# Nine full units a group of heads, and heads' rows laid out by DMA, in the first attention of a four-layer model

## The chip, the cores and the metric

The kernel runs on one core of a Trainium2 chip. The metric is the device time of one execution in microseconds. Before the change it is 3598.34 us, the median of three runs (3597.46 to 3599.22).

TensorE (PE) multiplies matrices and its weight loads are shown apart (PEld); VectorE is DVE, ScalarE is ACT, GpSimd is POOL; SyncE (SP) issues the DMAs. Everything is in float32, except one mask that is added by bfloat16 matmuls.

## The reference, cut to what matters

The model adds eight layers to x of 4 batches x 1024 positions x 128 features. The change lies in the first one, an attention with 16 heads of width 8, whose scores are a sum of four terms:

```python
v = (x @ v_w + v_b).reshape(Bq, Sq, H, Hd).transpose(0, 2, 1, 3)
...
scores = jnp.take(causal_kern, jnp.maximum(doff, 0), axis=-1)
qm = (x @ qmod_w + qmod_b).transpose(0, 2, 1)
km = (x @ kmod_w + kmod_b).transpose(0, 2, 1)
scores = scores + qm[..., :, None] + km[..., None, :]
qc = (x @ cq_w).reshape(Bq, Sq, H, CR).transpose(0, 2, 1, 3)
kc = (x @ ck_w).reshape(Bq, Sq, H, CR).transpose(0, 2, 1, 3)
scores = scores + MIX * jnp.einsum('bhic,bhjc->bhij', qc, kc) / math.sqrt(CR)
scores = jnp.where(causal, scores, -1000000000.0)
attn = jax.nn.softmax(scores, axis=-1)
ctx = jnp.einsum('bhij,bhjd->bhid', attn, v)
```

The first term depends on the distance of two positions alone (a table per head and batch). qm and km are one number per head and position, the modulations.

## The kernel before, in words

`attn0` first makes the table of the distance term (`position_table`), and then `attn0_heads` does the attention. A **group** is 4 heads of one batch, so there are 16 groups. Heads lie 32 rows apart: head h of a group has rows 32h to 32h+31 of a 128-row tile. Row 0 to 7 are the content of queries or keys, rows 8 and 9 the modulations against ones, and row 10 the shift of the softmax. So four matmuls of 32 rows each, one per head, run side by side on PE, and one product gives all of a score but the distance term.

The projections are therefore *gapped*: the weights `wq` and `wk` hold a head's 8 columns and its modulation in 32 columns with zeros between. For each group `queries(i)` (L669, evicted by ACT L671) and `keys(i)` (L675, L677) project the halves i = 0, 1 of 512 positions. Keys come from a transposed x with the positions reversed inside each half (`reverse`, `xr`), queries from a plain transpose (`turn`, `xT`).

The work of a group goes in **slots**. A slot has

- a *top*, which finds the maxima of scores without the distance term: four matmuls (L690 for the diagonal blocks, L705 for the others) into two pairs of PSUM banks, and two maximum reductions on DVE (L722). Diagonal blocks are masked first, by adding a lower value with the bfloat16 product of an identity and `after` (L698). The ten tops of a group are the list `tops`: both diagonals, `own` 3 and 7 (384 columns each), `both` 2 and 1 (a query tile in both halves; 512 and 256 columns), and four `before` (512). When a half's maxima are there, `maxima` is filled (L725), and `shift(i)` transposes it (L731) and adds it to the query rows (L732).
- *contract* of the unit three slots back (LAG = 3): the weights times the values (L787) into one bank, in which a whole half is summed and copied out by ACT at its end (L797).
- *weigh* of the unit nine slots back (LEAD = 9): scores of a key tile against all later queries of a half (L745) into two more pairs, the exponentials of heads 0 and 1 (L754) and of head 2 (L758) on ACT, the distance term of head 3 added on DVE (L757) ahead of its own exponential (L761). The other three heads get the distance term as a factor on POOL (L778), after a triangle is cut off in the diagonal block (L768). The ten units of a group are (0: 0), (0: 1 and 3), (0: 2), (1: 0) to (1: 4), (1: 5 and 7), (1: 6), written as half: key tiles. Eight have 512 columns, two have 256.
- *extras*, put into slots by hand with `at(slot, f)`: shift, queries, keys, for a new batch turn, reverse, values, and at a batch's end divide (L623 to L630), turn_back (L642), output (L649). All use the single bank `mm`, of which there is one.

PSUM has three pairs (tile `s`), one sum (`av`) and one single (`mm`). The order on PE, DVE and ACT is the written order (`manual_schedule`); POOL and SP are ordered by the framework. `fetch` loads a group's distance table (2 MB, two DMAs on SP, L665) in the first slot of the group into one of two buffers. Ahead of the slots, the first batch is transposed and the first group projected. What is left of the layer (`rest`) begins in the last slots.

Of the kernel before, what the change touches and what calls it, by code (L numbers as in the profile page):

```python
# [70 lines left out]
def gapped(w, width, at):  # L71

    k = w.shape[0]
    out = np.zeros((k, H, 32), np.float32)
    out[:, :, at : at + width] = w.reshape(k, H, width)
    return out.reshape(k, H * 32)


def head_columns(a):

    return np.asarray(a, np.float32).reshape(4, 4, 32).transpose(1, 2, 0).reshape(P, 4)


def layout(i):
# [41 lines left out]
    w.add("wq", gapped(a["cq_w"], 8, 0))  # L126
    w.parts[-1].reshape(P, H, 32)[:, :, 9] = a["qmod_w"]
    w.add("wk", gapped(a["ck_w"], 8, 0))
    w.parts[-1].reshape(P, H, 32)[:, :, 8] = a["kmod_w"]
    scale = np.ones((4, 32), np.float32)  # L130
    scale[:, :8] = 0.15 / np.sqrt(8.0)
    w.add("sq", scale.reshape(P, 1))
    bq = np.zeros((H, 32), np.float32)
    bq[:, 8] = 1.0
    bq[:, 9] = a["qmod_b"]
    w.add("bq", head_columns(bq))
    bk = np.zeros((H, 32), np.float32)
    bk[:, 8] = a["kmod_b"]
    bk[:, 9:11] = 1.0
    w.add("bk", head_columns(bk))  # L140
# [107 lines left out]
def hybrid_kernel(ctx: ExitStack, tc: tile.TileContext, x, out, blocks, dram, upto=8):  # L248
# [295 lines left out]
    def attn0_heads(W, xn, table, rest):  # L544
# [7 lines left out]
        LEAD, LAG = 9, 3  # L552

        tops = [("diagonal", 0), ("own", 3), ("both", 2), ("both", 1), ("diagonal", 1)]
        tops += [("before", it) for it in range(4, 8)] + [("own", 7)]

        units = [(i, jts) for i in range(2) for jts in [(jt,) for jt in range(4 * i + 1)] + [(4 * i + 1, 4 * i + 3), (4 * i + 2,)]]
        N = len(units)
        with layer_pool("a0h", 2) as pool, layer_pool("a0k", 1) as keep:

            maxima = [keep.tile([P, 4, P], F32, name=f"maxima{n}") for n in range(2)]
# [3 lines left out]
            parts = keep.tile([P, 2, 4, 4, 3], F32, name="parts")  # L565
            nc.gpsimd.memset(parts, -LOWEST)
            for n in range(2):
                nc.gpsimd.memset(maxima[n], 0.0)
                nc.gpsimd.memset(vals[n], 1.0)
# [14 lines left out]
            class Batch:  # L584
# [5 lines left out]
                def turn(self, i):  # L590
                    if i == 0:
                        self.xT = pool.tile([P, S], F32, name="xT", bufs=1)
                    ps = free()
                    for t in range(4):
                        nc.tensor.transpose(ps[:, t * P : (t + 1) * P], self.x[:, 4 * i + t, :], ident)
                    move(self.xT[:, i * 512 : (i + 1) * 512], ps)

                def reverse(self, i):

                    if i == 0:  # L600
                        self.xr = {}
                    ps = free()
                    for t in range(4):
                        mm(ps[:, (3 - t) * P : (4 - t) * P], self.x[:, 4 * i + t, :], flip, start=True, stop=True)
                    self.xr[i] = pool.tile([P, 512], F32, name=f"xr{i}", bufs=1)
                    move(self.xr[i], ps)
                    if i == 1:

                        nc.gpsimd.tensor_tensor(self.x, self.x, wide(shared, TB), ALU.add)
# [8 lines left out]
                def divide(self, t):  # L618
# [5 lines left out]
                    if t % 4 == 0:  # L624
                        self.o[i] = pool.tile([P, 4, H, 8], F32, name=f"o{i}", bufs=1)
# [13 lines left out]
                def turn_back(self, i):  # L639
# [3 lines left out]
                    self.oT[i] = pool.tile([P, 512], F32, name="oT")  # L643
# [9 lines left out]
            class Group:  # L653


                def __init__(self, batch, g):
                    self.batch, self.g = batch, g
                    self.q, self.k = {}, {}
# [8 lines left out]
                def queries(self, i):  # L667
                    ps = free()
                    mm(ps, W("wq")[:, self.g * P : (self.g + 1) * P], self.batch.xT[:, i * 512 : (i + 1) * 512], start=True, stop=True)  # L669
                    self.q[i] = pool.tile([P, 512], F32, name=f"q{i}")  # L670
                    nc.scalar.activation(self.q[i], ps, AF.Identity, bias=W("bq")[:, self.g : self.g + 1], scale=W("sq"))  # L671

                def keys(self, i):
                    ps = free()
                    mm(ps, W("wk")[:, self.g * P : (self.g + 1) * P], self.batch.xr[i], start=True, stop=True)  # L675
                    self.k[i] = pool.tile([P, 512], F32, name=f"k{i}")
                    nc.scalar.activation(self.k[i], ps, AF.Identity, bias=W("bk")[:, self.g : self.g + 1])  # L677

                def top(self, kind, n):
# [3 lines left out]
                    i = n if kind == "diagonal" else n // 4  # L683
                    t = n % 4
                    if kind == "diagonal":

                        for t in range(4):
                            for h in range(4):
                                r = slice(32 * h, 32 * h + 32)
                                mm(  # L690
                                    both[h // 2][:, h % 2, t * P : (t + 1) * P],
                                    self.q[i][r, t * P : (t + 1) * P],
                                    self.k[i][r, (3 - t) * P : (4 - t) * P],
                                    start=(t == 0),
                                    stop=False,
                                )
                        for h in range(4):
                            mm(both[h // 2][:, h % 2, :], ident16, wide(after, 4), start=False, stop=True)  # L698
                    else:
                        w = 512 if kind == "before" else t * P  # L700
                        for c, half in enumerate((0, 1) if kind == "both" else (i,)):
                            keys = self.k[0 if kind == "before" else half]
                            for h in range(4):
                                r = slice(32 * h, 32 * h + 32)
                                mm(  # L705
                                    both[h // 2][:, h % 2, c * w : (c + 1) * w],
                                    self.q[half][r, t * P : (t + 1) * P],
                                    keys[r, 512 - w : 512],
                                    start=True,
                                    stop=True,  # L710
                                )
                    for hp in range(2):
                        if kind == "diagonal":
                            o = parts[:, i, :, 2 * hp : 2 * hp + 2, 0].rearrange("p t h -> p h t")
                            x = both[hp].rearrange("p k (t w) -> p k t w", t=4)
                        elif kind == "both":
                            o = parts[:, :, t, 2 * hp : 2 * hp + 2, 1].rearrange("p i h -> p h i")
                            x = both[hp][:, :, 0 : 2 * w].rearrange("p k (i w) -> p k i w", i=2)
                        else:
                            o = parts[:, i, t, 2 * hp : 2 * hp + 2, 1 if kind == "own" else 2]  # L720
                            x = both[hp][:, :, 0:w]
                        nc.vector.tensor_reduce(o, x, AX.X, ALU.max, negate=True)  # L722
                    if (kind, n) in (tops[3], tops[-1]):
                        i = int((kind, n) == tops[-1])
                        nc.vector.tensor_reduce(maxima[i][:, :, 10:P:32], parts[:, i], AX.X, ALU.min)  # L725

                def shift(self, i):

                    ps = bank()
                    for t in range(4):  # L730
                        nc.tensor.transpose(ps[:, t * P : (t + 1) * P], maxima[i][:, t, :], ident)  # L731
                    return lambda: nc.vector.tensor_tensor(self.q[i], self.q[i], ps, ALU.add)  # L732

                def weigh(self, i, jts):

                    parted, w = [], 0
                    for jt in jts:
                        w0 = max(0, jt * P - 512 * i)
                        parted.append((jt, w0, slice(w, w + 512 - w0), 512 * i + w0 - jt * P))
                        w += 512 - w0  # L740
                    both = [pair().rearrange("p (k w) -> p k w", k=2) for _ in range(2)]
                    for jt, w0, c, u in parted:
                        for h in range(4):
                            r = slice(32 * h, 32 * h + 32)
# [11 lines left out]
                    for jt, w0, c, u in parted:  # L756
# [6 lines left out]
                    def bias():  # L763
                        for jt, w0, c, u in parted:
# [15 lines left out]
                    def contract():  # L780
                        ended = jts == (4 * i + 2,)
                        if jts[0] == 0:
                            self.acc = psum.sums()
                        for jt, w0, c, u in parted:
                            for h in range(4):
                                col = 16 * (4 * self.g + h)
                                mm(  # L787
                                    self.acc[32 * h : 32 * h + 32, w0:512],
                                    vals[self.batch.n][:, jt, col : col + 32],
                                    pt[:, h, c] if h < 3 else p3[:, c],  # L790
                                    start=(jt == 0),
# [1403 lines left out]
```

## Time and profile before

| | |
|---|---|
| time, median of three runs | 3598.34 us |
| the profiled execution: span from the first to the last instruction | 3593.0 us |
| what lies around the span (median less span) | 5.3 us |
| PE, DVE, ACT, POOL busy over the span | 95%, 57%, 55%, 26% |
| first top of the first group starts | 85.80 us |
| first exponential of the first unit (L754) starts | 112.47 us |
| last top reduced | 771.9 us |
| last first exponential starts | 808.35 us |
| L778 POOL, distance factor, 128x1536 (96 of the 192) | 3.44 us each |
| L722 DVE, maxima of 1024 columns | 1.21 us each, two a top |
| L754, L758, L761 ACT, 1024, 512, 512 columns | 1.02, 0.59, 0.63 us |
| L669, L675 PE, 60 projections in the slots, two instructions each | 1.02 to 1.12 us a projection |

The profiled execution has no time of its own beside its span; the three runs of the same kernel lie within 0.05% of each other. A line of the timeline reads: start, duration, engine, line, operation, what it writes and reads, shape, count of instructions, and in brackets how long the engine was idle before and who released it. Float32 matmuls are two instructions each, and four of them, on four groups of rows, run at the same time, so "x8, 1.07" is four matmuls of 512 columns side by side.

### The profile page before, as it was taken

To read this page: it belongs to the slowest core of one execution; us is meant where nothing else is said; L and a number is where in the kernel's file an instruction comes from. 1 tells how busy PE (TensorE), PEld (TensorE's weight loads), DVE (VectorE), ACT (ScalarE), POOL (GpSimd) and SP (SyncE) were. 2 spreads that over 40 slices of the span, in tenths; PEclk is the share of its full clock that TensorE was granted. 3 is DMA by queue.
4 is the path that set the end of the run, shared out by engine and by line. 5 is a ranking of instruction groups with operands and counts; after the bars stand their busy time and mean duration, and the time that the engine had idled before them with its cause. 6 is when DMAs were issued, how large, how long until landed. Compare 5 with 4: busy or idle time off the path is not lost.

```text
span 3593.0 us, 62577 instructions
## 1 busy us (share of the span) xinstructions
PE 3425.7 (95%) x25672; PEld 2041.0 (57%) x25672; DVE 2060.6 (57%) x4874; ACT 1959.1 (55%) x3284; POOL 916.5 (26%) x705
## 2 busy tenths in 40 slices
PE   7999999989999999999899999999999999999999
PEld 3444444436765566633333577666766766766777
DVE  5767767767644455577778411566566566566311
ACT  5455555556522225477677553566566566566543
POOL 4687878782022210122221000000001001000000
PEclk7999999999999999999999999999999999999999
DMA  3111111100520005200000000210010110100000
GB/s 98 50 48 48 48 48 48 48 24 23 147 61 1 1 15 142 72 1 1 1 1 1 14 1 1 72 36 29 32 36 25 36 36 25 36 25 24 4 10 13
DMA packets 95975, 124.34 MB, mean 35 GB/s; under 512 B 3660, under 2 KB 78028, under 8 KB 94536
## 3 DMA queue, kind: packets, MB, share of 16 engines
q1 hardware_dynamic: 95688, 120.33, 10.9%
q8 instruction: 202, 3.31, 0.4%
q14 instruction: 85, 0.70, 0.1%
HBM read 117.59 MB, written 2.73 MB: 33 GB/s over the span
## 4 chain that ended last, share of the span: by engine, by line
PE 83%; ACT 6%; DVE 6%; POOL 2%; DMA 1%; issue 1%; SPq 0%; ACTq 0%; DVEq 0%; POOLq 0%
PE mm L2040 8%; PE s L1990 8%; PE av L1827 6%; PE mm L1817 6%; PE av L2058 6%; PE s L745 5%; PE s L1653 4%; PE s L705 4%; PE av L787 4%; PE av L1148 3%; PE av L1687 3%; PE mm L1132 2%; ACT p L2025 2%; DVE p L1664 2%; PE av L1383 2%; PE mm L1347 2%
## 5 line engine op out<-in xcount | busy, mean ns | idle before, releaser
L778 POOL TENSOR_TENSOR p<-p,bias 128x1536 f32<-128x1536 f32 x192 | 503.2, 2629 | 64.5 <-ACT p L758 59.2
L2008 DVE CUSTOM_DVE_ANT_0 p<-s,bias 128x512 f32<-128x512 f32 (+3 forms) x768 | 387.0, 550 | 128.6 <-PE s L1990 121.5
L722 DVE TENSOR_REDUCE parts<-s 128x2 f32<-128x1024 f32 (+4 forms) x320 | 342.4, 1113 | 161.8 <-PE s L705 94.7
L2025 ACT ACTIVATE p<-p,tops 128x128 f32<-128x128 f32 (+7 forms) x512 | 395.2, 774 | 2.0 <-DVE tops L2008 1.8
L1664 DVE TENSOR_SCALAR p<-s 128x1024 f32<-128x1024 f32 (+1 forms) x320 | 340.8, 1110 | 82.3 <-PE s L1653 72.8
L2045 ACT COPY pt<-mm 128x512 f32<-128x512 f32 (+1 forms) x352 | 185.8, 528 | 364.2 <-PE mm L2040 364.0
L2040 PE MATMUL mm<-ident,p 128*128 128x128 f32 x2304 | 348.1, 283 | 30.7 <-ACT p L2025 30.3
L2040 PEld LDWEIGHTS mm<-ident,p 128*128 128x128 f32 x2304 | 248.3, 141 | 168.2 <-issue 63.4
L2073 POOL COPY wide_rec<-rec 128x512 f32<-128x512 f32 x64 | 39.4, 616 | 1163.0 <-DVE rec L2071 1098.7
L1667 ACT ACTIVATE p<-p 128x2048 f32<-128x2048 f32 (+1 forms) x160 | 277.6, 1740 | 93.7 <-DVE p L1664 93.1
L1827 PEld LDWEIGHTS av<-wt,hid 128*128 128x128 f32 x2048 | 263.9, 192 | 107.1 <-issue 107.1
L1990 PE MATMUL s<-keys,q 64*128 64x512 f32 (+3 forms) x1536 | 302.2, 512 | 4.5 <-DVE tops L2008 4.5
L754 ACT ACTIVATE p<-s 128x1024 f32<-128x1024 f32 (+1 forms) x160 | 150.3, 939 | 265.6 <-PE s L745 261.9
L2058 PE MATMUL av<-pt,vals 128*64 128x128 f32 x4608 | 294.7, 277 | 0.0
L1818 ACT ACTIVATE hid<-mm,wt 128x512 f32<-128x512 f32 x256 | 170.7, 690 | 219.2 <-PE mm L1817 218.9
L2058 PEld LDWEIGHTS av<-pt,vals 128*64 128x64 f32 x4608 | 248.4, 137 | 51.4 <-issue 40.8
L1827 PE MATMUL av<-wt,hid 128*128 128x128 f32 x2048 | 264.7, 275 | 0.0
L2047 DVE COPY pt<-mm 128x512 f32<-128x512 f32 (+1 forms) x288 | 189.6, 658 | 129.7 <-PE mm L2040 129.4
L1817 PE MATMUL mm<-xT,wt 128*128 128x512 f32 x512 | 260.2, 599 | 2.5 <-ACT hid L1818 2.0
L1653 PE MATMUL s<-q,k 32*128 32x512 f32 (+3 forms) x1536 | 209.9, 533 | 2.2 <-DVE p L1664 2.0
L745 PE MATMUL s<-q,k 32*128 32x512 f32 (+3 forms) x1536 | 197.4, 529 | 0.5 <-DVE parts L722 0.4
L1148 PEld LDWEIGHTS av<-wt,hid 128*128 128x128 f32 x1152 | 154.6, 200 | 60.5 <-issue 53.1
(405 smaller groups left out, 5282.4 us busy)
## 6 DMA issues: line engine op xcount, KB each, us to landing
root<-roots SPq DMA_DIRECT2D x128, 256.0 KB, 6.2
bias<-rel_dram SPq DMA_DIRECT2D x32, 1024.0 KB, 5.4
bias<-pos_dram SPq DMA_DIRECT2D x16, 1536.0 KB, 7.1
bias<-pos_dram SPq DMA_DIRECT2D x16, 512.0 KB, 7.9
wt<-w_ffn SPq DMA_DIRECT2D x2, 2132.0 KB, 8.0
wt<-w_ffn SPq DMA_DIRECT2D x2, 1192.0 KB, 5.2
wt<-w_attn SPq DMA_DIRECT2D x1, 2336.0 KB
x_sb<-x SPq DMA_DIRECT2D x4, 512.0 KB, 6.8
```

The costliest lines, as they stand in the source:

```text
L722: nc.vector.tensor_reduce(o, x, AX.X, ALU.max, negate=True)
L745: mm(both[h // 2][:, h % 2, c], self.k[jt // 4][r, (3 - jt % 4) * P : (4 - jt % 4) * P], self.q[i][r, w0:512], start=True, stop=True,)
L778: nc.gpsimd.tensor_tensor(d, d, self.bias[:, 0:3, u : u + 512 - w0], ALU.mult)
L1653: mm(both[h // 2][:, h % 2, c : c + 512 - w0], self.k[r, jt * P : (jt + 1) * P], self.q[r, 512 * i + w0 : 512 * (i + 1)], start=True, stop ...
L1664: nc.vector.tensor_scalar(pt[:, 2 * hp : 2 * hp + 2, 0:w], both[hp][:, :, 0:w], 80.0, -80.0, ALU.min, ALU.max)
L1817: mm(ps, W("w1")[:, c * P : (c + 1) * P], self.batch.xT[:, self.i * 512 : (self.i + 1) * 512], start=True, stop=True)
L1827: mm(o, self.hid[:, c, t * P : (t + 1) * P], W("w2")[:, c * P : (c + 1) * P], start=(c == 0), stop=(c == C - 1))
L1990: mm(s[:, kk, 0:e], self.q[r, it * P : (it + 1) * P], keys[self.n][r, S - n + c : S - n + c + e], start=True, stop=True,)
L2008: nc.vector.tensor_tensor_reduce(out=self.p[it][:, kk, c : c + e], in0=s[:, kk, 0:e], in1=self.bias[:, kk, c : c + e], scale=-1.0, scalar= ...
L2025: nc.scalar.activation(p, p, AF.Exp, bias=self.top[it][:, kk : kk + 1], scale=-1.0, accum_out=self.sums[:, it, kk : kk + 1])
L2040: nc.tensor.transpose(ps[:, m, kk, :], self.p[it][:, kk, (m0 + m) * P : (m0 + m + 1) * P], ident)
L2058: mm(self.acc[64 * kk : 64 * kk + 64, (it % 4) * P : (it % 4 + 1) * P], vals[self.n][:, it - m0 - m, :], pt[:, m, kk, :], start=(m0 + m == 0),
```

## The change

1. **Nine units and nine tops a group.** The half units are joined: (0: 2) and (1: 6) become one unit of 512 columns. The contraction of (1: 6) is held until the second half has been begun by (1: 0). The tops are cut by query tiles over whole causal rows: `row` is one tile's 512 columns, `rows` a tile of 384 and one of 128 columns, `both` two of 256 columns. Keys are reversed within a half, so the masked block is the first 128 columns of each piece, and masks are 128 columns wide for each. LEAD is 8.
2. **Content and modulations are projected without gaps**, once per batch and half: `compact` for queries and for keys (8 columns for each of the 16 heads), `modulate` for both modulations (two matmuls to 32 rows each).
3. **DMAs lay them into the head rows.** `Group.load(i)` issues 16 DMAs on SP for a half: per head 8 rows of query content, 2 rows (a modulation and a row of zeros), 8 rows of key content, one row. The target tiles `rows` are kept, two sets used in turn by odd and even groups, and are filled with ones once. Tops and weigh read 11 rows of each head and not 32.
4. The extras get new slots, one in each slot. `xT` shares the tile of the query content, `xr`, `o` and `oT` have one buffer for both halves, `maxima` one for both.

The core of the diff:

```diff
-        LEAD, LAG = 9, 3
+        LEAD, LAG = 8, 3
-        tops = [("diagonal", 0), ("own", 3), ("both", 2), ("both", 1), ("diagonal", 1)]
-        tops += [("before", it) for it in range(4, 8)] + [("own", 7)]
-        units = [(i, jts) for i in range(2) for jts in [(jt,) for jt in range(4 * i + 1)] + [(4 * i + 1, 4 * i + 3), (4 * i + 2,)]]
+        tops = [("row", 0), ("rows", 0), ("both", 1)] + [("before", it) for it in range(4, 8)] + [("row", 1), ("rows", 1)]
+        units = [((0, 0),), ((0, 1), (0, 3)), ((0, 2), (1, 6))] + [((1, jt),) for jt in range(5)] + [((1, 5), (1, 7))]
...
+                def compact(self, i, which):
+                    ps = free()
+                    cols = slice(i * 512, (i + 1) * 512)
+                    mm(ps, W("w" + which), self.xT[:, cols] if which == "q" else self.xr[i], start=True, stop=True)
+                    nc.scalar.mul(content[which][:, cols], ps, float(0.15 / np.sqrt(8.0)) if which == "q" else 1.0)
+                def modulate(self, i):
+                    ps = free()
+                    cols = slice(i * 512, (i + 1) * 512)
+                    for n, src in enumerate((self.xT[:, cols], self.xr[i])):
+                        mm(ps[32 * n : 32 * n + 32, :], W("mod")[:, 32 * n : 32 * n + 32], src, start=True, stop=True)
+                    nc.scalar.activation(mods[:, cols], ps[0:64, :], AF.Identity, bias=W("bmod"))
...
+                def load(self, i):
+                    cols = slice(i * 512, (i + 1) * 512)
+                    for h in range(4):
+                        head, r = 4 * self.g + h, 32 * h
+                        nc.sync.dma_start(self.q[i][r : r + 8, :], content["q"][8 * head : 8 * head + 8, cols])
+                        nc.sync.dma_start(self.q[i][r + 9 : r + 11, :], mods[2 * head : 2 * head + 2, cols])
+                        nc.sync.dma_start(self.k[i][r : r + 8, :], content["k"][8 * head : 8 * head + 8, cols])
+                        nc.sync.dma_start(self.k[i][r + 8 : r + 9, :], mods[32 + head : 33 + head, cols])
...
+                    if kind == "before":
+                        chunks = [(1, n % 4, 0, 512)]
+                    elif kind == "row":
+                        chunks = [(n, 3, 0, 512)]
+                    elif kind == "rows":
+                        chunks = [(n, 2, 0, 384), (n, 0, 384, 128)]
+                    else:
+                        chunks = [(0, 1, 0, 256), (1, 1, 256, 256)]
+                    for i, t, c, w in chunks:
+                        for h in range(4):
+                            r = slice(32 * h, 32 * h + 11)
+                            mm(
+                                both[h // 2][:, h % 2, c : c + w],
+                                self.q[i][r, t * P : (t + 1) * P],
+                                self.k[0 if kind == "before" else i][r, 512 - w : 512],
+                                start=(c == 0),
+                                stop=(kind == "before"),
+                            )
+                    if kind != "before":
+                        step = chunks[-1][2]
+                        for h in range(4):
...
+                            mm(o, ident16, wide(after, 2) if step else after, start=False, stop=True)
...
                 if k:
                     at(s, lambda v=group: v.fetch())
-                    at(s - 6, lambda v=group: v.queries(0))
-                    at(s - 4, lambda v=group: v.keys(0))
-                    at(s - 1, lambda v=group: v.queries(1))
-                    at(s - 2, lambda v=group: v.keys(1))
+                    at(s - 4, lambda v=group: v.load(0))
+                    at(s - 1, lambda v=group: v.load(1))
                 if k and group.g == 0:
...
+                        (-15, lambda v=batch: v.reverse(0)),
+                        (-14, lambda v=batch: v.values(0)),
+                        (-12, lambda v=batch: v.turn(0)),
+                        (-11, lambda v=batch: v.modulate(0)),
+                        (-10, lambda v=batch: v.compact(0, "q")),
+                        (-8, lambda v=batch: v.compact(0, "k")),
+                        (-7, lambda v=batch: v.reverse(1)),
+                        (-6, lambda v=batch: v.turn(1)),
+                        (-5, lambda v=batch: v.modulate(1)),
+                        (-3, lambda v=batch: v.compact(1, "q")),
+                        (-2, lambda v=batch: v.compact(1, "k")),
+                        (2, lambda v=batch: v.values(1)),
...
                     for i in range(2):
+                        first.reverse(i)
                         first.turn(i)
-                        first.reverse(i)
-                    for i in range(2):
-                        groups[0].queries(i)
-                        groups[0].keys(i)
-                    for i in range(2):
+                        first.modulate(i)
+                        first.compact(i, "q")
+                        first.compact(i, "k")
+                        groups[0].load(i)
                         first.values(i)
                     groups[0].fetch()
```

## The prediction, made before the change was run

> **What bounds the kernel now.** I read the windows first, then the timeline of one slot, then the groups. Windows over the stage of the change (from the first exponential to the last slot with a top), then over what follows:
>
> ```profile
> 112.47:775.15 662.68, 645.32 (x5695) 283.04 (x5691) 466.44 (x645) 354.89 (x564) 537.86 (x304) 1.00 0.14 46
> 775.15:820.00 44.85, 30.93 (x232) 11.96 (x231) 16.13 (x39) 26.04 (x46) 40.38 (x22) 0.85 0.00 1
> ```
>
> The columns are length, then PE, PEld, DVE, ACT, POOL busy, PE clock, DMA. PE is busy 97%, POOL 81%, the clock is full. One slot in the timeline shows what kind of busy it is:
>
> ```profile
> 713.41 1.03 ACT L754 ACTIVATE p<-s 128x1024 f32<-128x1024 f32 x1 [1.68 <-PE s L745]
> 713.60 0.66 PE L731 MATMUL mm<-ident,maxima 128*128 128x128 f32 x4
> 714.18 1.43 PE L705 MATMUL s<-k,q 32*128 32x512 f32 x8
> 715.36 2.36 DVE L722 TENSOR_REDUCE parts<-s 128x2 f32<-128x1024 f32 x2 [0.29 <-PE s L705]
> 715.54 1.07 PE L787 MATMUL av<-p,vals 128*32 128x512 f32 x8
> 716.54 1.23 PE L745 MATMUL s<-q,k 32*128 32x512 f32 x8
> 717.77 1.02 ACT L754 ACTIVATE p<-s 128x1024 f32<-128x1024 f32 x1 [2.15 <-PE s L745]
> ```
>
> With three pairs of banks, the second half of a top (heads 2, 3) gets the pair that L754 is still reading. So a slot is a ring: exponential until +1.08 us, heads 2 and 3 of the top, the contraction from +2.13, weigh from +3.13, next exponential at +4.36. An extra of 0.66 us (here L731) lies under the exponential and costs nothing. I call the time from one start of L754 to the next a period, and took all 159 from the timeline. An undisturbed group (687.22 to 730.59) has, by top: diagonal 5.40, own 3 3.32, both 2 3.96, both 1 3.98, diagonal 4.96, before 4.57, 4.37, 4.49, 3.97, own 7 4.36; sum 43.37. The last group, where no projection follows, shows before 4.38 and 4.37 without one, and own 7 3.72. The 15 groups from 112.47 to 775.15 average 44.18, since where a divide shares the one single bank with a keys projection the period is 5.97 for 4.49 and 5.37 for 4.36.
>
> **The change, part by part.** All against this execution's span, 3593.0; the median of the runs is 3598.34, 5.3 higher, and I add that back at the end.
>
> *Projections leave the groups.* Beyond the bare period q0 costs 4.57 - 4.38 = 0.19, k0 4.49 - 4.37 = 0.12, k1 4.36 - 3.72 = 0.64, q1 unknown (0 taken). That is 0.95 a group, 14.3 us over 15. The collisions with divides go too, since each slot after gets one extra: group spans 44.84 and 45.84 against 43.37, so 1.47 + 2.47 = 3.94 at each of three batch changes, 11.8 us. Together 26 us.
>
> *Ten tops and units become nine.* The columns are equal: tops 2x512 + 2x384 + 512 + 256 + 4x512 = 4608 = 9x512, units 9x512 too. So only a slot's ring can be saved, and it is then full in every slot. Bare periods of before sum to 5.40+3.32+3.96+3.98+4.96+4.38+4.37+4.37+3.95+3.72 = 42.41. For after I build them from the ring. Four tops "before": 4.37. The five others add masks between the top and the contraction, here at a diagonal:
>
> ```profile
> 704.96 1.16 PE L690 MATMUL s<-k,q 32*128 32x128 f32 x28 [0.18 <-ACT p L754]
> 706.05 1.04 PE L698 MATMUL s<-after,ident 128*128 128x512 bf16 x4
> 706.69 2.36 DVE L722 TENSOR_REDUCE parts<-s 128x8 f32<-128x1024 f32 x2 [2.07 <-PE s L698]
> 707.01 0.64 PE L787 MATMUL av<-p,vals 128*32 128x256 f32 x8
> ```
>
> Four masks of 512 columns hold the contraction back by 0.97, 0.24 each. Masks of 128 and 256 columns are not in the trace. They lie between 0.06 and 0.12 (by columns) and 0.24 (as these); I take 0.10 and 0.12, because the weight load that goes with each mask takes 0.098 (L698, PEld), which is the nearest row. So "row" is 4.37 + 0.40 = 4.77. "rows" has 384 columns (0.84, L705 at own 3) and 128 (0.30, two passes of the diagonal) for 1.07, then 4x0.12: 4.93. "both" is 4.86. Sum: 4x4.37 + 2x4.77 + 2x4.93 + 4.86 = 41.74, and 0.1 more for the held part of unit (1, 6), whose contraction moves from one slot to the next. So 41.84 against 42.41: 0.57 a group, 8.5 us.
>
> *Extras added.* From the second batch on reverse, values, output, modulate and compact (12 a batch) keep PE 1.0 to 1.16 us, longer than the 0.9 that hides; by q0 and k0 each costs 0.12 to 0.19. 36 x 0.15 = 5.4 us given back. Of the twelve, values cost 0.21 to 0.25 before as well, so this is not low.
>
> *Row loads.* 32 DMAs a group on SP, which had two. The trace has no copy between SBUF tiles. Nearest are the four stores of 16 rows at L530 and, far above in descriptors, the spreading at L1105:
>
> ```profile
> L530 SPq DMA_DIRECT2D pos_dram<-wt x4: 303/360/413, 76.6 to 79.0; - x4
> DMA to landing us min/median/max: 2.0/2.3/2.5
> ```
>
> ```profile
> L1105 SPq DMA_DIRECT2D root<-roots x128: 359/864/2953, 900.9 to 1461.3; - x128
> DMA to landing us min/median/max: 5.0/6.2/7.6
> ```
>
> 8 rows of 2 KB are nearer to 16 rows of 4.6 KB, so 0.36 to issue and 2.3 to land; with 0.05 for a wait, 16 take 6.6 + 2.3 = 8.9 us. load(0) stands in slot s - 4 and waits for the keys of group g - 2 that unit (1, 3) reads in that very slot; the first top of g comes three periods and 0.5 later, about 14.6 us. load(1), free from s - 2, is due in the second chunk of "both" at s + 2. Both fit. The bias fetch is queued behind load(1) on SP and is needed eight slots on. At a batch change turn(0) (ACT, s - 12) overwrites the content that load(0) of slot s - 13 still reads: 13 DMAs and a landing, 7.6 us, against 6.3 until the copy; 1.3 of wait on ACT, which idles 1.7 to 2.2 before L754; I count 2 us for three changes. What does not hide is PE's waiting on so many DMAs. A top meets up to 4 per head, 16 per load; an extra wait is an event of 51 ns on PE's queue (L675, 9 of them), so 0 to 0.8 per load, 0 to 1.6 a group. Most pass while PE waits for the exponential; I take 0.3 a group, 4.5 us.
>
> [...]
>
> *Start.* The first top ran at 85.80 and the first exponential at 112.47, with DVE at work for 21.2 of the 26.7. Nine tops in full cost DVE 9 x 2.36 + 0.6 for the split "rows", 21.8: the same. But the first top now waits for rows. Keys of the first half are projected at about 82; 16 issues and a landing end at 90.9 and the second half 6.6 later. The weight transfer of the next layer (issued 81.48) may stand in front. I take 6 us later, bounds 2 and 12.
>
> *Tail.* After the last top the time is set by POOL (40.4 of 44.9 us) and by a table change on ACT; POOL's multiplies are the same. 0.
>
> POOL's work a group stays 35.7 (units from 3.44 to 4.67), under 42.5, so it does not take over.
>
> **Sum.** -26 - 8.5 + 5.4 + 4.5 + 2 + 6 = -16.6 (a group of about 42.5). Profiled span 3593.0 - 16.6 = 3576.4; as a time 3598.3 - 16.6 = 3581.7, rounded to **3582**.
>
> **Rivals.**
> 1. *PE is bound by its work.* Against it the ring; for it 97% busy. Then 60 projections within the stage at 1.06 go, 18 (12 compact, 6 modulate) come: 42 x 1.06 = 45 us less, 3554. With the collisions gone and cheap masks 3560 is in reach. Chance 0.10.
> 2. *The saving is eaten by waits and masks.* Masks at 0.16 and 0.20 add 2x0.24 + 3x0.32 = 1.4 a group, 22 us: 3604; PE's DMA waits at 0.8 a load add 1.3 a group, 20 us: 3602. Either, or half of both, ends within 0.2% of before. Against: the load of 0.098 and the exponential that covers the waits. Chance 0.18.
> 3. *Slower: the rows arrive late.* If one row DMA holds SP 0.86 us as at L1105, load(0) takes 16.1 of 14.6 and load(1), behind it, ends some 4.4 after its due time: 6 a group, 96 us, 3678. It decides from 0.77 us per DMA on, waits included. A smaller form is a late start and ACT held at each batch change, 12 and 12 us, with rival 2's masks: 3612. For it: order on SP is not written by hand, and nothing in the trace copies between tiles. Against: L530. Chance 0.25, most of it in the smaller form.
>
> That 11 rows do not run four abreast is excluded: L412, with slices of 3 rows, runs twelve of 512 columns in 1.99 us, where a full array takes 0.43 for each.
>
> **How the numbers follow.** My forecast, 3565 to 3592, has 0.47. Faster by over 0.2% (7.2 us, about what a measurement can tell) is forecast plus rival 1, 0.57; within 0.2% 0.18; slower 0.25. The forecast's own range is 3565 to 3592; the range of eight in ten reaches over rival 2 and the smaller form of rival 3: 3560 to 3613.
>
> **What would show it.** Periods at "before" tops of 4.37, at masked tops of 4.75 to 4.95, nine to a group, and a group near 42.5; six projections a batch where sixteen stood; SP issues near 0.36 us; no top waiting on a DMA. I am wrong in the ring if "before" periods fall below 4.2; in masks if the contraction stands over 0.7 behind the top; in rows if a top names a DMA as its releaser, or if the first exponential is later than 124.

## The result, and the profile after

The changed kernel takes 3875.83 us (median of four runs, 3856.95 to 3884.85), beside 3597.90 for the kernel before (four runs, 3596.83 to 3599.22): a ratio of 1.077, interval 1.0745 to 1.0795. The forecast was 3582, and 3613 the upper end of its range. The sign and the size were both wrong.

The profiled execution took 3867.15 us, with a span of 3864.9. From its page, the clock row and the three groups of matmuls in the slots (busy us, mean ns of one):

```profile
span 3864.9 us, 62253 instructions
...
PEclk9556765766699999899999999999999999999999
...
L693 PE MATMUL s<-rows_k,rows_q 11*128 11x512 f32 (+3 forms) x1536 | 328.7, 752 | 8.3 <-ACT p L750 5.2
...
L741 PE MATMUL s<-rows_q,rows_k 11*128 11x512 f32 (+3 forms) x1536 | 257.3, 740 | 1.7 <-ACT p L750 1.7
L782 PE MATMUL av<-p,vals 128*32 128x512 f32 (+3 forms) x1536 | 246.9, 757 | 7.7 <-POOL p L774 7.6
```

The same two rows of the kernel before:

```profile
PEclk7999999999999999999999999999999999999999
...
L745 PE MATMUL s<-q,k 32*128 32x512 f32 (+3 forms) x1536 | 197.4, 529 | 0.5 <-DVE parts L722 0.4
```

The second to eleventh of the 40 slices of the clock row are the attention. They read 9 in the kernel before and 5 to 7 here, and 9 again in the layers after it (one slice reads 8). Weigh (L741) takes 740 ns a matmul, where the same 1536 (L745 of before) took 529. The contraction (L782) takes 757, and its matmuls were not edited.

The windows that answer to those of the prediction, first exponential to the first exponential of the sixteenth group (15 groups), then to the last first exponential:

```profile
131.91:1039.74 907.83, 902.59 (x5060) 364.36 (x5060) 470.42 (x673) 317.34 (x477) 535.76 (x303) 0.63 0.13 40
1039.74:1071.44 31.70, 26.08 (x190) 9.48 (x187) 15.26 (x22) 22.77 (x37) 28.05 (x16) 0.78 0.00 1
```

The sixth column of numbers, behind the five engines, is the clock: 0.63, where it was 1.00. DVE, ACT and POOL are busy for 470, 317 and 536 us, where it was 466, 353 and 536; PE alone grew, from 643 to 903. The 15 groups take 907.83 for 660.53, 60.5 each for 44.0. That is 247 of the 272 us that the span gained; 19 more lie ahead of the first exponential (131.91 for 112.47), and 9 after the last one, less 4 that the last group saved.

One slot of "before" in the timeline, which answers to the slot in the prediction:

```profile
957.18 1.02 ACT L750 ACTIVATE p<-s 128x1024 f32<-128x1024 f32 x1 [5.98 <-PE s L741]
...
958.03 2.30 PE L693 MATMUL s<-rows_k,rows_q 11*128 11x512 f32 x8
...
960.16 2.36 DVE L718 TENSOR_REDUCE parts<-s 128x2 f32<-128x1024 f32 x2 [1.33 <-PE s L693]
...
960.26 1.94 PE L782 MATMUL av<-p,vals 128*32 128x512 f32 x8
...
962.13 2.09 PE L741 MATMUL s<-rows_q,rows_k 11*128 11x512 f32 x8
...
964.25 1.02 ACT L750 ACTIVATE p<-s 128x1024 f32<-128x1024 f32 x1 [5.05 <-PE s L741]
```

It is the same ring, at a "before" top. But contraction and weigh take 1.94 and 2.09 for 1.07 and 1.23, so the period is 7.07, where the prediction had 4.37. Nothing waits longer for a transfer; PE itself runs at half speed. The windows give this stretch a clock of 0.50 and the one from 993 to 995 us, inside the same stage, 1.00. The 94 clock records of this trace hold these two values only, in stretches of 3.41 us and multiples of it (the last one ends with the trace).

### The profile page after: what moved, and what is told of

It is laid out like the page before. It is cut to its first block, busy times and chain, and to the rows that moved or that the text cites. A ratio compares the mean times of both kernels' runs of the same rounds, so it can differ in the third digit from the quotient of the medians.

```text
span 3864.9 us, 62253 instructions
## 1 busy us (share of the span) xinstructions
PE 3710.3 (96%) x25032; PEld 2132.0 (55%) x25032; DVE 2071.4 (54%) x4906; ACT 1920.9 (50%) x3196; POOL 917.4 (24%) x712
## 4 chain that ended last, share of the span: by engine, by line
PE 85%; ACT 6%; DVE 4%; POOL 2%; DMA 1%; issue 1%; SPq 1%; ACTq 0%; DVEq 0%; POOLq 0%
PE mm L2051 8%; PE s L693 8%; PE s L2001 7%; PE s L741 6%; PE av L1838 6%; PE av L782 6%; PE mm L1828 6%; PE av L2069 5%; PE s L1664 4%; PE av L1159 3%; PE av L1698 3%; PE mm L1143 2%; ACT p L2036 2%; DVE p L1675 2%; PE av L1394 2%; PE mm L1358 2%
## 5 line engine op out<-in xcount | busy, mean ns | idle before, releaser
L774 POOL TENSOR_TENSOR p<-p,bias 128x1536 f32<-128x1536 f32 (+1 forms) x192 | 501.3, 2622 | 175.7 <-ACT p L754 173.1
L718 DVE TENSOR_REDUCE parts<-s 128x2 f32<-128x1024 f32 (+1 forms) x320 | 306.8, 1005 | 215.0 <-PE s L709 137.4
L750 ACT ACTIVATE p<-s 128x1024 f32<-128x1024 f32 x144 | 147.4, 1024 | 551.5 <-PE s L741 551.5
L693 PE MATMUL s<-rows_k,rows_q 11*128 11x512 f32 (+3 forms) x1536 | 328.7, 752 | 8.3 <-ACT p L750 5.2
L1838 PEld LDWEIGHTS av<-wt,hid 128*128 128x128 f32 x2048 | 263.9, 192 | 107.1 <-issue 107.1
L741 PE MATMUL s<-rows_q,rows_k 11*128 11x512 f32 (+3 forms) x1536 | 257.3, 740 | 1.7 <-ACT p L750 1.7
L782 PE MATMUL av<-p,vals 128*32 128x512 f32 (+3 forms) x1536 | 246.9, 757 | 7.7 <-POOL p L774 7.6
```

Source lines behind the costliest of these rows:

```text
L693: mm(both[h // 2][:, h % 2, c : c + w], self.q[i][r, t * P : (t + 1) * P], self.k[0 if kind == "before" else i][r, 512 - w : 512], start=( ...
L741: mm(both[h // 2][:, h % 2, c], self.k[jt // 4][r, (3 - jt % 4) * P : (4 - jt % 4) * P], self.q[i][r, w0:512], start=True, stop=True,)
L774: nc.gpsimd.tensor_tensor(d, d, self.bias[:, 0:3, u : u + 512 - w0], ALU.mult)
L782: mm(self.acc[32 * h : 32 * h + 32, w0:512], vals[self.batch.n][:, jt, col : col + 32], pt[:, h, c] if h < 3 else p3[:, c], start=(jt == 0 ...
L1838: mm(o, self.hid[:, c, t * P : (t + 1) * P], W("w2")[:, c * P : (c + 1) * P], start=(c == 0), stop=(c == C - 1))
```

## The experiments

Four theories were told apart. **Rows**: reading 11 rows of each 32 lowers the granted clock. **Waits**: the new order with its many DMA waits breaks PE's work up, and the clock falls for that. **Data**: it matters what lies in the rows. **Issue** (for the start alone): the first exponential is late because of 32 row DMAs on SP. Each kernel was timed beside the kernel before on the same chip.

### The change, reading 32 rows

```diff
-  r = slice(32 * h, 32 * h + 11)
+  r = slice(32 * h, 32 * h + 32)     # in the tops and in weigh
```

> The changed kernel, but tops and weigh read all 32 rows of a head; rows 11 to 31 are ones on both sides, which adds 21 to every score of a row and cancels in the softmax. Rows theory (the granted clock follows how many rows of the array the matmuls use, and 11 of 32 are too few): the clock in the stage goes back from about 0.63 to above 0.95, periods at the fast values seen inside the changed kernel (sum 42.5 a group), and the time is 3580 to 3600: the 3582 of the prediction plus up to 14 us for the later start. Waits theory (the new order makes PE wait, and the clock falls for that): the clock stays near 0.63 and the time stays near 3870.

Measured: 3597.88 us, ratio 0.9996 (0.9987 to 1.0005). Its 15 groups, clock third from the end:

```profile
129.37:772.16 642.79, 638.88 (x5056) 293.20 (x5052) 464.85 (x672) 320.27 (x476) 535.89 (x302) 0.99 0.19 57
```

Every DMA and wait of the change is still there, the clock is back at 0.99 and the loss is gone. Rows holds, waits falls.

### The kernel before, reading 11 rows

```diff
-  r = slice(32 * h, 32 * h + 32)
+  r = slice(32 * h, 32 * h + 11)     # L689, L704, L744 of the kernel before, nothing else
```

> The kernel before, with only the slices of its tops and weigh cut from 32 to 11 rows (rows 11 to 31 are zeros there, so nothing else changes). Rows theory: the clock in the stage falls below 0.8 and the time rises by 150 to 300 us, to 3750 to 3900. Waits theory: it stays at 3598 with the clock at 0.98, since its order and its waits are those of before.

Measured: 3933.94 us, ratio 1.0924 (1.0894 to 1.0954). Three slices, and the old kernel loses more than the change did, and 34 us more than the upper end of what was expected. The instructions and the values that count are the same; rows 11 to 31, no longer read, hold zeros. The 15 groups of this kernel, in the windows (clock third from the end):

```profile
117.77:1117.08 999.31, 984.36 (x5666) 375.70 (x5666) 469.96 (x644) 352.88 (x560) 536.89 (x303) 0.59 0.09 30
```

Against the kernel before, in its own window of 15 groups:

```profile
112.47:773.00 660.53, 643.17 (x5666) 281.68 (x5666) 465.75 (x644) 352.86 (x561) 536.46 (x303) 1.00 0.14 46
```

The reader should see 5666 matmuls in both, the times of DVE, ACT and POOL equal within 1%, and 0.59 against 1.00.

### Zeros in the spare rows

On top of the edit of the first experiment, which reads 32 rows in the tops and in weigh:

```diff
-  nc.gpsimd.memset(t, 1.0)
+  nc.gpsimd.memset(t, 0.0)
+  for h in range(4):
+      nc.gpsimd.memset(t[32 * h : 32 * h + 11, :], 1.0)
```

> The changed kernel with 32 rows, but rows 11 to 31 hold zeros on both sides. Rows theory: as with ones, clock above 0.95 and 3580 to 3600, because the rows count and not what is in them. Data theory (the clock follows what the rows hold): the clock falls to between 0.6 and 0.9 and the time lies over 3650. Waits theory: near 3870.

Measured: 3595.64 us, ratio 0.9987 (0.9978 to 0.9996), against 3597.88 with ones. The data theory falls: rows of zeros hold the clock as well as rows of ones. This kernel is the change as it was meant, with its clock full, so the steps of the prediction are judged on it. Its windows: to the first exponential, 15 groups, and to the last exponential.

```profile
85.00:128.25 43.25, 36.82 (x158) 17.16 (x156) 22.12 (x25) 3.43 (x6) 2.35 (x1) 0.72 0.30 90
128.25:768.58 640.33, 635.37 (x5056) 291.59 (x5056) 465.87 (x674) 320.28 (x476) 535.96 (x302) 1.00 0.19 57
768.58:800.25 31.67, 23.28 (x191) 8.27 (x190) 14.96 (x24) 22.69 (x37) 29.27 (x18) 0.90 0.01 2
```

### How many rows, and in which matmuls

The four are edits of the same two slices: 20 rows in both (beside ones), 16 in both, 11 in the tops alone, 11 in weigh alone (beside zeros).

```diff
-  r = slice(32 * h, 32 * h + 32)
+  r = slice(32 * h, 32 * h + 20)     # or 16; or 11 in one of the two places
```

> The changed kernel with 20 rows of a head read (ones in rows 11 to 19). Rows theory: between the two, clock and time from its place between 11 and 32 rows; if it is a threshold, either above 0.95 and near 3590 or still under 0.75 and over 3780. Waits theory: near 3870.

> Tops and weigh read 16 rows. Rows theory with a mark between 11 and 20: the clock in the stage lies between 0.63 and 0.95, and the time between 3640 and 3860; if the mark is sharp, at one of these ends.

> The 32 rows with zeros, but the tops read 11 rows and weigh reads 32. If the clock follows the rows averaged over all matmuls of some microseconds: the mean over tops and weigh is 21.5, so near the 20 rows of before: clock in the stage above 0.93, 3600 to 3640. If one kind of matmul under the mark is enough: clock under 0.75, over 3780.

> As the run beside it, but weigh reads 11 rows and the tops read 32. By the average: the same clock and time as with the tops cut, within 30 us. If one kind under the mark is enough: under 0.75 and over 3780.

| rows in tops, weigh | time, us | ratio, interval | 15 groups, us | clock in them |
|---|---|---|---|---|
| 32, 32 (zeros) | 3595.64 | 0.9987 (0.9978 to 0.9996) | 640.33 | 1.00 |
| 20, 20 | 3619.08 | 1.0075 (1.0045 to 1.0104) | 656.23 | 0.97 |
| 11, 32 | 3616.93 | 1.0052 (1.0034 to 1.007) | 659.16 | 0.96 |
| 32, 11 | 3629.13 | 1.0086 (1.0068 to 1.0104) | 677.67 | 0.93 |
| 16, 16 | 3699.53 | 1.0282 (1.0263 to 1.03) | 747.25 | 0.81 |
| 11, 11 (the change) | 3875.83 | 1.077 (1.0745 to 1.0795) | 907.83 | 0.63 |

The entries with 16 rows and with 11 in one place rest on two runs each; the nine runs with 20 rows spread from 3611.77 to 3657.61. The last two columns are from one profiled execution each. The window of 16 rows, for its shape:

```profile
128.65:875.90 747.25, 743.24 (x5056) 322.92 (x5052) 467.73 (x672) 318.52 (x476) 535.40 (x302) 0.81 0.16 49
```

PE is busy 99% of it, and 99% of the window with 32 rows. What falls is the clock, by degrees with the rows that are read. 11 rows in one kind of matmul cost 0.5 or 0.9% of the kernel before, 20 in both 0.75%, which fits an average over both kinds (11 and 32 make 21.5). That one kind below some mark is enough for the whole loss is refuted by these rows.

### The first group projected as before

From the kernel with zeros; several lines are joined in the cut. Group 0 alone gets gapped weights and no row DMAs; the content that later groups need is projected partly ahead, partly as extras of the first four slots.

```diff
-  first.modulate(i); first.compact(i, "q"); first.compact(i, "k"); groups[0].load(i)
+  groups[0].project(i)               # two gapped projections into rows
   first.values(i)
+  if i == 0: first.modulate(i); first.compact(i, "k")
...
+  at(0, lambda: batches[0].compact(0, "q"))
+  at(1, lambda: batches[0].modulate(1))
+  at(2, lambda: batches[0].compact(1, "q"))
+  at(3, lambda: batches[0].compact(1, "k"))
```

> The 32 rows with zeros, and the first group alone projected with gaps as in the kernel before (no row DMAs for it; modulations and content of the first batch are projected after or beside that). Issue theory (what is left of the gain is lost at the start, since a row DMA holds SP 0.55 to 0.77 us and the first group's 32 stand in front of its tops): the first exponential comes at 112 to 118 instead of 128.3, and the time falls by 10 to 15 us to 3580 to 3587. Rival (the start is set by the new order of the prologue on PE and by the half clock there, not by the DMAs): the first exponential stays after 124 and the time at 3592 to 3597.

Measured: 3583.74 us (3583.53 to 3587.84) beside 3597.77, ratio 0.9963 (0.9949 to 0.9976). It is faster than the kernel before by 0.4%, and so than the change. Its first exponential and its 15 groups:

```profile
115.67 1.02 ACT L784 ACTIVATE p<-s 128x1024 f32<-128x1024 f32 x1 [14.98 <-PE s L775]
```

```profile
115.67:758.34 642.67, 638.19 (x5056) 292.90 (x5052) 465.02 (x672) 320.26 (x476) 535.78 (x302) 0.99 0.19 56
```

The start comes 12.6 us earlier (115.67 for 128.25) and the groups stay. The edit takes away the row DMAs of the first group, but also shortens what PE does ahead of the first top, so the share of each is read from the timelines. The first reduction of a top begins at 90.89 here and at 100.40 in the kernel with zeros, 9.5 us apart. PE's last projection ahead of it ends at 89.56 here and at 91.85 there, so some 2.3 us are the shorter prologue and some 7.2 the first top, which waits for its rows there. The last 3 us lie behind that; there the kernel with zeros runs at 0.72 (85 to 128.25 us), and this one shows 0.82 from 0 to 115.67, a window with the prologue in it, so the clock's share of the 3 is not shown.

## Why the prediction was wrong, step by step

**The clock (the step that failed).** The prediction read "the clock is full" in the first window and took it as given for the new one. Its one sentence on the 11 rows, "That 11 rows do not run four abreast is excluded", asks whether they run side by side. They do: in a stretch at full clock (from 286.6 us) the changed kernel's four "before" periods are 4.39, 3.96, 4.89 and 4.31, and with 32 rows their medians are 4.39, 3.96, 4.82 and 4.30. It didn't ask what reading fewer rows does to the clock. The row that it leaned on (L412, slices of 3 rows) could not tell: its window from 60 to 66 us is at 1.00, the whole stretch from 0 to 85.8 at 0.78 with idle time in it. The term had no measured bound, and no rival had it. The term that was left at 0 is 907.83 - 640.33 = 267.5 us in 15 groups. Reading 32 rows in the change takes the loss away, and reading 11 in the old kernel brings it.

**The ring and the groups: right.** Without the start, the terms gave 660.5 - 26 - 8.5 + 5.4 + 4.5 + 2 = 637.9 us for 15 groups; 640.33 was measured. The periods with the zeros, as medians by top: row 4.86 and 4.82 (predicted 4.77), rows 4.95 and 4.91 (4.93), four "before" 17.47 together (17.58 with the held part), both 5.41 (4.86). The four are 4.39, 3.96, 4.82 and 4.30, so one lies under the 4.2 that was named as a sign against the ring. It is the held contraction: in the group at 693 us its slot contracts for 0.64 us and the next one for 1.50, where others take 1.07, and the two periods together come to 8.78 for twice 4.37. One slot, which answers to that of the prediction (a period of 4.30):

```profile
712.17 1.02 ACT L752 ACTIVATE p<-s 128x1024 f32<-128x1024 f32 x1 [2.79 <-PE s L743]
...
712.57 1.80 PE L695 MATMUL s<-rows_k,rows_q 32*128 32x512 f32 x8
...
713.74 2.36 DVE L720 TENSOR_REDUCE parts<-s 128x2 f32<-128x1024 f32 x2 [0.19 <-PE s L695]
...
714.30 1.06 PE L784 MATMUL av<-p,vals 128*32 128x512 f32 x8
...
715.30 1.14 PE L743 MATMUL s<-rows_q,rows_k 32*128 32x512 f32 x8
...
716.47 1.02 ACT L752 ACTIVATE p<-s 128x1024 f32<-128x1024 f32 x1 [2.27 <-PE s L743]
```

**PE's waits on DMAs: within the bounds, nearly twice the term, and in one slot.** "Both" is the top that first touches the second half's rows:

```profile
693.58 1.02 ACT L752 ACTIVATE p<-s 128x1024 f32<-128x1024 f32 x1 [0.54 <-PE s L743]
...
694.29 1.98 PE L695 MATMUL s<-rows_k,rows_q 32*128 32x256 f32 x16
...
696.20 0.61 PE L711 MATMUL s<-after,ident 128*128 128x256 bf16 x4
...
696.74 1.07 PE L784 MATMUL av<-p,vals 128*32 128x512 f32 x8
...
698.99 1.02 ACT L752 ACTIVATE p<-s 128x1024 f32<-128x1024 f32 x1 [2.65 <-PE s L743]
```

The masks begin 2.62 after the exponential, where the ring lets them begin at about 2.13. PE's queue holds nine semaphore events of 0.05 us in that gap, and no wait of PE in the 15 groups names a DMA. So it is 0.55 a group against 0.3, within the bounds of 0 and 1.6; that the events make all of it is read from the lines and was not tried by itself. The lines show the masks as well: four of 256 columns hold the contraction back by 0.54 (predicted 0.48).

**Long extras and batch changes: less than thought.** A plain group spans 42.41, so 15 are 636.15, and all else, the first group included, is 4.2 us, where 5.4 + 2 had been put.

**The row DMAs: mis-sized.** 0.36 to issue came from stores of 16 rows to DRAM. In the kernel with zeros, min, median and max in ns of three of the four kinds (2, 8 and 1 rows; one line from each of three views):

```profile
L669 SPq DMA_DIRECT2D rows_q<-mods x128: 587/587/605, 85.4 to 729.9; - x128
...
L670 SPq DMA_DIRECT2D rows_k<-content_k x128: 624/644/673, 86.1 to 730.5; - x128
...
L671 SPq DMA_DIRECT2D rows_k<-mods x128: 547/547/1587, 87.4 to 731.2; - x128
```

With the gap between them a DMA holds SP about 0.65. That is under the 0.77 from which rival 3 decides: 16 take some 10.5 us, and load(0) has 14.6. So rival 3 didn't happen in the groups. It did at the start, where nothing hides it. In the timeline the first tops name the DMAs as their releaser, one of the two signs against the rows that the prediction gave; the other, a first exponential later than 124, came as well:

```profile
93.22 1.32 PE L695 MATMUL s<-rows_k,rows_q 32*128 32x512 f32 x4 [1.36 <-DMA rows_k<-mods]
...
95.42 1.09 PE L695 MATMUL s<-rows_k,rows_q 32*128 32x512 f32 x2 [0.87 <-DMA rows_k<-mods]
...
97.99 2.04 PE L695 MATMUL s<-rows_k,rows_q 32*128 32x512 f32 x2 [1.49 <-DMA rows_k<-mods]
...
108.54 1.19 PE L695 MATMUL s<-rows_k,rows_q 32*128 32x256 f32 x2 [0.73 <-DMA rows_k<-mods]
```

The second half's DMAs end at 107.3, and the broken-up work runs at a clock of 0.72. The first exponential is 15.8 us later than before (128.25 for 112.47), where 6 was predicted and 12 was the bound.

**Tail: two errors of opposite sign.** From the sixteenth group's first exponential to the last one 3.7 us are saved (31.67 for 35.35), which fits a LEAD of 8 for 9, but wasn't tried by itself. After the last exponential 10.1 us are added (2794.75 for 2784.65). About 5 of them lie in the rest of this layer: the last exponential comes 8.1 us earlier than in the kernel before (800.25 for 808.35), and L994 in what is left of the layer (L981 of before) only 2.9 (824.82 for 827.76). The other 5 build up behind that, in work that no edit touches. From the last exponential to the end PE is busy 2681.93 us, for 2674.70, and in four windows of that stretch the clock reads 0.97, 0.98, 1.00 and 1.00 in both kernels. Executions of the kernel before alone spread from 3591.67 to 3603.13, so this part stays open.

**The sum.** With the clock held, the span moves by 15.8 - 20.2 - 3.7 + 10.1 = 2.0 us, and the groups' gain is paid back by the start and the tail. With the start mended it is 3.2 - 17.9 - 5.0 + 8.5 = -11.2 in the span and 14 in the median (3583.74 for 3597.77), near the -16.6 of the prediction, and not for all of its reasons. The table took what lies around the span as 5.3 us. In the runs that have both numbers it is 1.7 to 2.3, so the profiled execution of before was itself some 3 us faster than the median.

**Slips.** "The 15 groups average 44.18" took the wrong end; to the sixteenth group's first exponential it is 660.53 / 15 = 44.04. No term of the sum uses it. The smaller form of rival 3 adds up, by the terms that it names, to some 3620 and not 3612; the measured time lies far outside either.

**The rivals.** Rival 1 falls: at full clock the "before" periods average 4.37, as the ring has it, so PE's amount of work does not set them. Rival 2 names about the time of the kernel with 32 rows, but masks and waits came out near the main forecast; it was the start and the tail that ate the gain. Rival 3 had the sign of the result and not its cause; of its smaller form the late start happened.

## What to carry to other kernels

Where PE is busy nearly all the time, a matmul that needs few rows of a row group should still read all 32, with zeros in the spare ones: here that costs no time (ratio 0.9987), and leaving them out cost 8 to 9% of the whole kernel (1.077 and 1.0924). Any edit of a slice in a stage that is bound by PE asks for a term for the granted clock, and the windows by stage show it at once. Many small DMAs can lie beside steady work at 0.65 us of SP each, but the first set stands on the path of the start; project that one directly.

## What the runs showed of the hardware that was not expected

- The granted clock follows the rows that are read, at a PE that is 98 to 99% busy in each case: 1.00 at 32 of 32 rows, 0.97 at 20, 0.81 at 16, 0.63 at 11 (0.59 in the kernel before). At 32 rows zeros count as much as ones (1.00 and 0.99). It is gradual in the mean between 11 and 20 rows, though in the records of the changed kernel every stretch is at 0.5 or 1.0.
- How much of the time PE is busy does not tell the two apart. In the changed kernel's groups PE is busy 41.07 of the 41.07 us from 131.91 to 172.98, at a clock of 0.50, and 30.70 of the 30.72 from 285.62 to 316.34, at 1.00. What takes the clock from one to the other inside a kernel, and at how many rows, was not shown; the runs have the means alone.
- At a clock of 0.50 work that was not edited takes longer too: the contraction, which reads all 128 rows, takes 1.94 us (at 960.26 in the changed kernel), for 1.07 at 1.00.
- A DMA of 1, 2 or 8 rows holds SP for 0.55, 0.59 or 0.64 to 0.65 us, longer than the 0.36 of the store of 16 rows at L530. That one goes to DRAM and has longer rows (4.6 KB for 2), so the count of rows is not shown to be the reason.
